# A reordered ending in a fused ViT tower: one layer and a top-2 mixture of experts on one core

## The chip, the core and the metric

The kernel runs on one core of a Trainium2 chip. A core has a matrix engine (TensorE, "PE" in the profile, with its weight loads listed as "PEld"), VectorE ("DVE"), ScalarE ("ACT"), GpSimd ("POOL"), and SyncE ("SP"), which here only starts transfers. The engines run their own instruction streams and wait for one another through semaphores. The metric is the time of one execution on the device in microseconds (us). Before the change it is 2110.49 us, the median of 3 runs from 2110.33 to 2110.68.

## What is computed

The reference, cut to what matters (biases and the small helper functions left out):

```python
# x: (4, 64, 512, 64) = batch, channel, time, series
patches = windows of 16 steps, stride 8, edge-padded by 8      # 64 per series
xf = rfft(patches, norm='ortho')                               # 9 frequencies
h = concat(xf.real, xf.imag) @ W.T                             # (4, 4096, 256)

# layer 0, on a = layernorm(h)
n = layernorm(a);  q, k, v = n @ Wq.T, n @ Wk.T, n @ Wv.T
mem_t = 0.9 * mem_(t-1) + k_t * v_t                            # along the tokens
a = a + q * mem
h = h + a + relu(layernorm(a) @ W1.T) @ W2.T                   # 256 -> 1024 -> 256

# mixture of experts, on tok = layernorm(h)
probs = softmax(tok @ router.T);  the two largest of 8, renormalised
h = h + tok + sum over the two of  weight * (gelu(tok @ w1[e]) @ w2[e])
```

There are 4 x 4096 = 16384 tokens of 256 features, all in float32.

## The kernel before

**Blocks.** The tokens are cut into 32 blocks of 512 (`BLK`; `NS` = 31 is the number of the last). A loop over `i` = 0 to 30 works on three blocks at once: `new` (block i: embedding, first norm, q/k/v, the scan that is called retention, the residual), `mid` (block i-1: the MLP, that is `mlp_in(m)` for eight slices of the hidden layer and `mlp_out` for two halves of the tokens, then the norm that gives `tok`) and `old` (block i-2: the router, then the scattering of its tokens). A written-out ending after the loop (L1287 on) does what is left: block 31 (`last`) from its embedding, block 30 (`mid`) from its MLP, block 29 (`old`) from its router, and the experts of all of them.

**Router and token lists.** `rows` copies a block's tokens into rows with tag fields, `logits` (TensorE) and `choose` (VectorE) find the two best experts, `place` computes for every token the two places in per-expert lists, and `scatter` has POOL write the rows to a buffer in DRAM, `xbuf`: eight indirect transfers per block, two per group of 128 tokens. `scatter(n)` writes up to group n, so a block's scatters can be spread.

**Expert tiles.** After a block's rows are placed, `take(n, block, writes)` (VectorE) makes tiles from the full lists: 256 rows of one expert each. The schedule of tiles is fixed: `take(29)` makes tiles 105 to 108 in the last round of the loop (from block 28), `take(30)` tiles 109 to 112 (block 29) and `take(31)` the last 18, tiles 113 to 130, partly filled (block 30). There are 131. Each passes these methods of class `Tile`:

- `load` (L960): SP starts three transfers: the expert's weights `w` (641.5 KB, at a row read from the table of `take`), the tile's rows transposed as `xh` (DMA_TRANSPOSE) and their tags `xg`. SP waits for the table and for the scatters before them. For the last block's tiles the weights are not loaded (L963).
- `fetch` (L982): for just those tiles, a copy of the expert's weights out of the `bank` in SBUF into `w`, by VectorE for even tiles of a `take` and by ScalarE for odd ones.
- `turn` (L991): ScalarE puts the two halves of the transposed rows together as `xT` (two copies, L995).
- `enter` (L997): eight matmul records on TensorE into PSUM (L1002), then two GELUs by ScalarE (L1010).
- `leave` (L1014): eight matmul records (L1019). `sums` (L1027): VectorE adds the bias and scales by the router's weights, and POOL adds the rows into the output by indirect transfers (L1048).

`expert_step` (`expert_halves` in two parts) runs one step of this small pipeline: `load` of the tile four ahead, `turn` of the next (which is the one that enters in the following step), `enter`, `leave` and `sums` of the one before, `fetch` of the tile four ahead. `slot_halves` (L1158) is the loop's form of it: it does nothing unless more than `LEFT` = 3 tiles stand before `enter`. Weights have five buffers, `xh` six, `xT` two, and the PSUM tiles that `enter` shares with transposes (`p_mm`) two.

**The bank.** All eight experts' weights (8 x 641.5 KB) are loaded once more in the ending, into SBUF that the embedding no longer needs. `load_bank` (L938) is a generator: each `next(weights)` starts one load on ScalarE's own queue. Before the change these stand at the MLP products m = 1, 3, 5 and 7 of block 30, after the last of these products, after `place` of block 29, after the first half of block 30's output product, and after `take(30)`. Block 31's tokens never go through lists: for it, each expert runs over the whole block straight from the bank (class `Expert`, L1081 and L1098), between the remaining tiles.

**What sets the order.** For SP, TensorE, VectorE and ScalarE the order of instructions is the order in which the code is written (`manual_schedule`); POOL's order is the planner's. An instruction that waits therefore holds up everything written behind it on its engine. Where line 305 and line 306 appear, they are `to_features`: four TensorE transposes per half of a block, and the copy out of PSUM by ScalarE. Line 767 is the exponential of `choose` for block 31. Line 608 is the transposes of `residual`.

Of the kernel before, what the change touches and what calls it, by code (L numbers as in the profile page):

```python
# [16 lines left out]
AF = mybir.ActivationFunctionType  # L17
# [19 lines left out]
def vit_tower_kernel(  # L37
# [23 lines left out]
    TT = 4  # L61
# [288 lines left out]
    class Block:  # L350
# [381 lines left out]
        def choose(self):  # L732

            ps = self.lg
            shape = [P, TT, E]

            def wide(a):
                return a.unsqueeze(2).to_broadcast(shape)

            lg = small.tile(shape, F32, name="lg")  # L740
            top = small.tile([P, TT], F32, name="top")
            if self.i == NS:
                first_key = small.tile([P, TT], F32, name="first_key")
            else:
                first_key = self.row.bitcast(F32)[:, :, FIRST]
            turned = small.tile([P, TT, G], F32, name="turned_lg")
            nc.vector.transpose(turned.rearrange("p t g -> p (t g)"), ps.rearrange("p t g -> p (t g)"))
            nc.vector.tensor_reduce(top, turned[:, :, :E], AX.X, ALU.max)
            nc.vector.tensor_tensor(lg, turned[:, :, :E], wide(top), ALU.subtract)
            key = small.tile(shape, F32, name="key")  # L750
            self.oh = oh = small.tile([P, 2, TT, E], F32, name="oh")
            nc.vector.scalar_tensor_tensor(key, lg, 0.0, key0, ALU.is_equal, ALU.mult)
            nc.vector.tensor_reduce(first_key, key, AX.X, ALU.max)
            nc.vector.tensor_tensor(oh[:, 0], key, wide(first_key), ALU.is_equal)
            nc.vector.scalar_tensor_tensor(lg, oh[:, 0], -3.0e38, lg, ALU.mult, ALU.add)
            second = small.tile([P, TT], F32, name="second")
            nc.vector.tensor_reduce(second, lg, AX.X, ALU.max)
            nc.vector.tensor_tensor(key, lg, wide(second), ALU.is_equal)
            nc.vector.tensor_tensor(key, key, key0, ALU.mult)
            nc.vector.tensor_reduce(top, key, AX.X, ALU.max)  # L760
            nc.vector.tensor_tensor(oh[:, 1], key, wide(top), ALU.is_equal)
            dtype = F32 if self.i == NS else BF16
            self.both = small.tile(shape, dtype, name=f"both_{dtype.name}")
            nc.vector.tensor_tensor(self.both, oh[:, 0], oh[:, 1], ALU.add)
            self.ex = small.tile([P, TT], F32, name="ex")
            if self.i == NS:
                nc.scalar.activation(self.ex, second, AF.Exp)
            else:
                nc.gpsimd.tensor_tensor(self.ex, euler, second, ALU.pow)

# [7 lines left out]

        def combine(self):

            diff = small.tile([P, TT], F32, name="diff")
            second = small.tile([P, TT], F32, name="second")
            self.weights(diff, second)
            shape = [P, TT, E]
            self.share = self.both
            nc.vector.tensor_tensor(self.share, self.both, second.unsqueeze(2).to_broadcast(shape), ALU.mult)
            first = self.oh[:, 0]
            nc.vector.tensor_tensor(first, first, diff.unsqueeze(2).to_broadcast(shape), ALU.mult)
            nc.vector.tensor_tensor(self.share, self.share, first, ALU.add)
# [68 lines left out]
    def take(n, block, writes):  # L858
# [40 lines left out]
        expert = small.tile([P, KMAX], F32, name="expert")[:, :k]  # L899
        nc.vector.tensor_reduce(expert, past, AX.X, ALU.add)  # L900
        table = four.tile([P, 2, KMAX], I32, name="table")[:, :, :k]
        if block.i >= NS - 1:
            nc.vector.tensor_scalar(table[:, 0, :], expert, float(E - 1), None, ALU.min)
        else:
            nc.vector.tensor_scalar(table[:, 0, :], expert, float(P), float((E - 1) * P), ALU.mult, ALU.min)
# [47 lines left out]
    class Tile:  # L953
# [6 lines left out]
        def load(self):  # L960
            t = self.t
            self.w = five.tile([P, NW], F32, name="w")
            if self.block.i < NS - 1:  # L963
                wrow = nc.sync.value_load(self.table[:, 0, t : t + 1], min_val=0, max_val=(E - 1) * P)
                nc.sync.dma_start(out=self.w, in_=wex[bass.ds(wrow, P), :])

            def rows():
                row = nc.sync.value_load(self.table[:, 1, t : t + 1], min_val=0, max_val=ROWS - S)
                return xbuf[bass.ds(row, S), :]

            self.xh = six.tile([P, 2 * KD, S], U16, name="xh")
            read = nc.sync.dma_start(out=self.xh, in_=rows().bitcast(U16)[:, : 2 * D], transpose=True)
            unordered("rows", read, self.writes)
            self.xg = twelve.tile([P, 2, RW - D], I32, name="xg")
            read = nc.sync.dma_start(out=self.xg, in_=rows()[:, D:].rearrange("(c p) d -> p c d", p=P))
            unordered("rows", read, self.writes)
# [3 lines left out]
            return self.block.put == TT  # L980

        def fetch(self):  # L982
            if self.block.i >= NS - 1:

                assert len(loaded) == E
                t = self.t
                engine, copy = ((nc.vector, nc.vector.tensor_copy), (nc.scalar, nc.scalar.copy))[t % 2]
                e = engine.value_load(self.table[:, 0, t : t + 1], min_val=0, max_val=E - 1)
                copy(self.w.unsqueeze(1), bank[0][:, bass.ds(e, 1), :])
# [157 lines left out]
    def run(steps):  # L1147
        for _ in steps:
            pass

    def expert_step(**how):
        run(expert_halves(**how))
# [2 lines left out]

    LEFT = 3

    def slot_halves(known, load=True, sums=True):  # L1158

        if len(tiles) - at["enter"] > LEFT and at["enter"] + 2 <= known:  # L1160
            yield from expert_halves(load=load, sums=sums)

    def slot(known, load=True):
# [8 lines left out]
    with tc.manual_schedule(engines=MANUAL):  # L1172
# [3 lines left out]
        for i in range(NS):  # L1176
# [54 lines left out]
            if i:  # L1231
                qkv = new.qkv()
                if old:
                    old.logits()
                    old.choose()
                if i >= EARLY:
                    next(ahead)
                next(qkv)
                next(qkv)
                tile_steps = slot_halves(known, sums=False)  # L1240
                next(tile_steps, None)
                next(qkv)
                if old:
                    writes = old.place(at_once=False)
                    old.scatter(1)
                run(tile_steps)
                if old:
                    old.scatter(2, last_product[0])
                next(qkv)
                advance("sums", at["leave"])  # L1250
                later = slot_halves(known, load=False)
                next(later, None)
                next(qkv)
                new.first_norm()
                for m in range(KD):
                    new.scan(m)
                if EARLY <= i < NB - 2:
                    xs[i + 2] = load_x(i + 2)
                mid.mlp_out(0)
                if old:  # L1260
                    old.scatter(3, last_product[0])
            else:
                xs[i + 2] = load_x(i + 2)
                new.first_norm()
                for m in range(KD):
                    new.retention(m)
# [42 lines left out]
        next(weights)  # L1309
        old.logits()  # L1310
        old.choose()
        expert_step()
        writes = old.place()
        next(weights)
        restore_weights()
        last.first_norm()
        last.retention(0)
        mid.mlp_out(0)
        next(weights)
        take(NS - 1, old, writes)  # L1320
        next(weights)
        mid.mlp_out(1)
        last.retention(1)
        beside = expert_halves(fetch=False)
        next(beside)
        mid.features3()
        mid.rows()
        advance("leave", at["enter"] - 1)
        mid.logits()
        mid.choose()  # L1330
        run(beside)
        expert_step(fetch=False, sums=False)
        writes = mid.place()
        advance("sums", at["leave"])
        expert_step(fetch=False, sums=False)
        last.residual()
        expert_step(fetch=False, sums=False)
        advance("sums", at["leave"])
        expert_step(fetch=False)
        take(NS, mid, writes)  # L1340

        last.features2()
        expert_step(turn=False)
        mid.store()
        last.sum_up()
        for m in range(KH):
            last.mlp_in(m)
            if m == TT - 1:
                advance("turn", at["enter"] + 1)
            if m == KH - 3:  # L1350
                expert_step()
        expert_step()
        last.mlp_out(0, expert_step)
# [107 lines left out]
```

## Time and profile before

| | us |
|---|---|
| median of 3 runs | 2110.49 |
| the profiled execution | 2116.49 |
| its span, first to last instruction | 2114.7 |
| stretch of the loop, 0 to 1853: TensorE busy | 1832.66 of 1853.00 |
| 1853 to 1950 (first part of the ending): TensorE busy | 88.75 of 97.00 |
| 1950 to 2015: TensorE busy | 60.94 of 65.00 |
| 2015 to the end: TensorE busy | 95.00 of 99.70 |
| TensorE's granted clock in these four | 1.00, 0.95, 0.97, 1.00 |
| share of time that the DMA engines were busy in these four | 0.61, 0.81, 0.67, 0.44 |

The profile is of one execution, which took 2116.49 us; all times read in it belong to that one, and they are counted from its first instruction. "Busy" is time in which an engine worked on an instruction; a matmul record that runs at a lower clock is busy longer. The granted clock is the share of full speed at which the chip ran TensorE in that stretch. In a timeline a line has the start and the duration in us, the engine, the source line, the instruction, what it writes and reads, and in square brackets the time for which the engine stood idle before it and what ended that: "<-ACT xT L995" is the instruction of ScalarE at line 995 that wrote `xT`, and "<-issue" means that the profile shows nothing that was waited for. In the tables of stretches each engine has its busy time and its number of instructions in the order PE, PEld, DVE, ACT, POOL; after these stand the granted clock, the DMA share and GB/s. In the stretch from 1853 to 2015 the groups with most idle time before them on TensorE are the tiles' first products:

```profile
L1002 PE MATMUL mm<-xT,w 128*128 128x256 f32 x144 | 38.0, 410 | 6.9 <-ACT xT L995 3.8 <-ACT hT L306 2.4 <-issue 0.7
L1019 PE MATMUL tm<-w,ge 128*128 128x256 f32 x144 | 35.1, 388 | 0.0
```

Here the numbers after the count are the group's busy time in us, the mean of one record in ns, the idle time before the group's records, and the three kinds of release that ended most of it.

### The profile page before, as it was taken

To read this page: it belongs to the slowest core of one execution; us is meant where nothing else is said; L and a number is where in the kernel's file an instruction comes from. 1 tells how busy PE (TensorE), PEld (TensorE's weight loads), DVE (VectorE), ACT (ScalarE), POOL (GpSimd) and SP (SyncE) were. 2 spreads that over 40 slices of the span, in tenths; PEclk is the share of its full clock that TensorE was granted. 3 is DMA by queue.
4 is the path that set the end of the run, shared out by engine and by line. 5 is a ranking of instruction groups with operands and counts; after the bars stand their busy time and mean duration, and the time that the engine had idled before them with its cause. 6 is when DMAs were issued, how large, how long until landed. Compare 5 with 4: busy or idle time off the path is not lost.

```text
span 2114.7 us, 30454 instructions
## 1 busy us (share of the span) xinstructions
PE 2077.4 (98%) x9042; PEld 1576.0 (75%) x9042; DVE 1674.8 (79%) x5179; ACT 1100.8 (52%) x1966; POOL 886.9 (42%) x768
## 2 busy tenths in 40 slices
PE   8999999999999999999999999999999999998999
PEld 5777677777777777777777777787777787676776
DVE  6778888888888888888888888888888888767445
ACT  2344455655545565554556555455665545543453
POOL 1032234444444444544444444444444444535444
PEclk9999999999999999999999999999999999999999
DMA  4031256766676676567667766766776567688653
GB/s 142 4 123 64 80 131 138 160 143 129 134 157 146 155 160 139 125 143 159 156 143 160 150 122 136 157 156 143 163 157 118 138 149 161 138 197 168 91 69 50
DMA packets 424519, 283.21 MB, mean 134 GB/s; under 512 B 355104, under 2 KB 391072, under 8 KB 420256
## 3 DMA queue, kind: packets, MB, share of 16 engines
q1 hardware_dynamic: 373424, 208.35, 42.5%
q0 software_dynamic: 49632, 67.39, 17.8%
q10 hardware_dynamic: 1296, 5.52, 0.8%
q8 instruction: 71, 1.16, 0.2%
q14 instruction: 96, 0.79, 0.1%
HBM read 118.36 MB, written 86.52 MB: 97 GB/s over the span
## 4 chain that ended last, share of the span: by engine, by line
PE 74%; DVE 11%; ACT 5%; DMA 5%; issue 2%; POOL 2%; SPq 1%; another core or an unknown queue 0%; ACTq 0%; DVEq 0%; POOLq 0%
PE tm L650 17%; PE sums L339 13%; PE tm L396 9%; PE sums L524 9%; PE mm L1002 8%; PE tm L1019 8%; DMA turned<-planes 3%; DVE st L263 2%; PE mm L540 1%; ACT planes L318 1%; ACT tokT L332 1%; PE tm L1098 1%; PE mm L1081 1%; PE mm L539 1%; SPq L326 1%
## 5 line engine op out<-in xcount | busy, mean ns | idle before, releaser
L1048 POOL DMA_INDIRECT out<-y,xg x226 | 369.2, 1634 | 432.7 <-DVE y L1038 220.2
L650 PE MATMUL tm<-w_sb,aT 128*128 128x256 f32 x2048 | 454.7, 380 | 0.0
L339 PE MATMUL sums<-hT,w_sb 128*128 128x512 f32 x1024 | 451.7, 593 | 1.3 <-ACT aT L640 1.3
L650 PEld LDWEIGHTS tm<-w_sb,aT 128*128 128x128 f32 x2048 | 386.7, 190 | 57.2 <-DVE z L611 4.8
L819 POOL DMA_INDIRECT xbuf<-row,to x248 | 257.1, 1037 | 294.3 <-DVE ks L560 170.5
L339 PEld LDWEIGHTS sums<-hT,w_sb 128*128 128x128 f32 x1024 | 193.4, 190 | 219.9 <-issue 201.0
L396 PE MATMUL tm<-wu,xv 128*128 128x256 f32 x1280 | 282.5, 379 | 0.0
L318 ACT COPY planes<-zz 128x1024 uint16<-128x1024 uint16 x100 | 99.3, 1041 | 342.0 <-DVE zz L292 342.0
L396 PEld LDWEIGHTS tm<-wu,xv 128*128 128x128 f32 x1280 | 242.7, 190 | 32.7
L1002 PE MATMUL mm<-xT,w 128*128 128x256 f32 x1048 | 252.5, 384 | 6.9 <-ACT xT L995 3.8
L1019 PE MATMUL tm<-w,ge 128*128 128x256 f32 x1048 | 253.4, 385 | 0.0
L1002 PEld LDWEIGHTS mm<-xT,w 128*128 128x128 f32 x1048 | 201.3, 193 | 49.9 <-issue 16.0
L1019 PEld LDWEIGHTS tm<-w,ge 128*128 128x128 f32 x1048 | 195.9, 191 | 31.4 <-issue 2.9
L640 ACT ACTIVATE aT<-sums,vec 128x512 f32<-128x512 f32 x256 | 167.0, 690 | 60.6 <-PE sums L339 59.3
L995 ACT COPY xT<-xh 128x512 uint16<-128x512 uint16 x262 | 182.1, 767 | 24.4 <-DMA xh<-xbuf 15.4
L283 POOL TENSOR_SCALAR rstd<-mv 128x4 f32<-128x4 f32 x62 | 42.0, 678 | 333.2 <-DVE mv L264 296.7
L1010 ACT ACTIVATE ge<-mm,w 128x256 f32<-128x256 f32 x262 | 109.9, 474 | 137.5 <-PE mm L1002 76.3
L1036 DVE TENSOR_TENSOR y<-tm,w 128x512 f32<-128x512 f32 x131 | 90.6, 691 | 97.9 <-PE tm L1019 86.6
L332 ACT COPY hT<-turned 128x512 uint16<-128x512 uint16 x100 | 66.2, 762 | 80.5 <-DMA turned<-planes 80.5
L263 DVE BATCH_NORM_STATS2 st<-h 128x6 f32<-128x256 f32 x256 | 104.8, 409 | 3.3
L332 ACT COPY tokT<-turned 128x512 uint16<-128x512 uint16 x116 | 76.5, 760 | 58.7 <-DMA turned<-row 58.7
L524 PE MATMUL sums<-hT,wqkv_sb 128*128 128x256 f32 x360 | 107.1, 379 | 0.0
(224 smaller groups left out, 3105.4 us busy)
## 6 DMA issues: line engine op xcount, KB each, us to landing
w<-in_wex SPq DMA_DIRECT2D x113, 641.5 KB
xb<-in_x SPq DMA_DIRECT2D x32, 1040.0 KB
out<-h SPq DMA_DIRECT2D x31, 512.0 KB
bank<-in_wex ACTq DMA_DIRECT2D x8, 641.5 KB
xbuf<-row,to POOLq DMA_INDIRECT x248
out<-y,xg POOLq DMA_INDIRECT x226
xh<-xbuf SPq DMA_TRANSPOSE x131
xg<-xbuf SPq DMA_DIRECT2D x131, 4.0 KB
```

Of the source, the lines that this page charges most:

```text
L263: nc.vector.bn_stats(self.st[:, t, :], src[:, t, :])
L332: copy(to[:, 1 - i], self.turned[:, :, i, k, :])
L339: nc.tensor.matmul(ps, lhsT=w[:, k, ts(m, P)], rhs=rhs[:, k, :], start=k == 0, stop=k == KD - 1)
L396: nc.tensor.matmul(ps[:, n, :], lhsT=xv[:, i, j, :], rhs=wu[:, i, j, :], start=j == 0, stop=j == J - 1)
L524: nc.tensor.matmul(g[:, n, :], lhsT=lhsT, rhs=rhs, start=False, stop=True, skip_group_check=True)
L640: nc.scalar.activation(self.aT[:, m, :], ps, AF.Relu, bias=vec[:, MB1 + m : MB1 + m + 1])
L650: last_product[0] = nc.tensor.matmul(ps[:, i, :], lhsT=self.aT[:, k, ts(u * 2 + i, P)], rhs=w2_sb[:, k, :], start=k == 0, stop=k == KH - 1,)
L819: write = nc.gpsimd.indirect_dma_start(out=xbuf, out_offset=bass.IndirectOffsetOnAxis(ap=self.to[:, c, t : t + 1], axis=0), in_=self.row[: ...
L995: nc.scalar.copy(halves[:, :, :, 1 - i], self.xh[:, i * KD : (i + 1) * KD, :])
L1002: nc.tensor.matmul(ps[:, m, :], lhsT=self.w[:, k * D + m * P : k * D + (m + 1) * P], rhs=self.xT[:, k, :], start=k == 0, stop=k == KD - 1,)
L1019: last_product[0] = nc.tensor.matmul(ps[:, c, :], lhsT=self.ge[:, k, ts(c, P)], rhs=w[:, (2 + k) * D : (3 + k) * D], start=k == 0, stop=k ...
L1048: add = nc.gpsimd.indirect_dma_start(out=out, out_offset=bass.IndirectOffsetOnAxis(ap=number[:, c, :], axis=0), in_=y[:, c, :], in_offset= ...
```

## The change

**The exponential.** For block 31, `choose` only keeps `second`, and `combine` begins with the exponential of it.

**Block 29's tiles.** In `take`, `load` and `fetch` the limit `NS - 1` becomes `NS - 2`: tiles 109 to 112 no longer load their weights from DRAM in `load`, and copy them from the bank in `fetch`.

**One more tile in the loop's last round.** `slot_halves` gets a parameter `left`. In round 30 its last use (`later`) takes `LEFT - 1`, so that a tile enters there which before entered in the ending.

**The ending's order.** In block 29's part, the tile between `choose` and `place` goes; block 31's first norm and first half of the retention move ahead of `place`. The second half of the retention moves into block 30's first output product (between its two groups of 128 tokens), and block 31's residual into the second one. After it come a tile, `features2` of block 31 (its transposes), a tile, the first MLP product of block 31, block 30's router with tiles and block 31's second MLP product between its steps, and `take(31)`. Block 30's rows are scattered in two parts. The other six MLP products of block 31 follow, with a tile and `store` and `sum_up` at the fourth, `turn` at the seventh and a tile at the eighth. Before, block 31's residual and `features2` came after `place` of block 30, with four tiles around, and all eight products after `take(31)`.

**The bank's loads.** The first five and the sixth stay at the same calls (m = 1, 3, 5, 7, after the products, after `place` of block 29); the seventh stands after the second half of the retention and the eighth before `take(30)`, where it was behind.

```diff
@@ choose @@
             if self.i == NS:
-                nc.scalar.activation(self.ex, second, AF.Exp)
+                self.second = second
@@ combine @@
+            nc.scalar.activation(self.ex, self.second, AF.Exp)
             diff = small.tile([P, TT], F32, name="diff")
@@ take @@
-        if block.i >= NS - 1:
+        if block.i >= NS - 2:
             nc.vector.tensor_scalar(table[:, 0, :], expert, float(E - 1), None, ALU.min)
@@ Tile.load @@
-            if self.block.i < NS - 1:
+            if self.block.i < NS - 2:
                 wrow = nc.sync.value_load(self.table[:, 0, t : t + 1], min_val=0, max_val=(E - 1) * P)
                 nc.sync.dma_start(out=self.w, in_=wex[bass.ds(wrow, P), :])
@@ Tile.fetch @@
-            if self.block.i >= NS - 1:
+            if self.block.i >= NS - 2:
@@ slot_halves @@
-    def slot_halves(known, load=True, sums=True):
-        if len(tiles) - at["enter"] > LEFT and at["enter"] + 2 <= known:
+    def slot_halves(known, load=True, sums=True, left=LEFT):
+        if len(tiles) - at["enter"] > left and at["enter"] + 2 <= known:
             yield from expert_halves(load=load, sums=sums)
@@ the loop @@
-                later = slot_halves(known, load=False)
+                later = slot_halves(known, load=False, left=LEFT - (i == NS - 1))
@@ the ending @@
         old.logits()
         old.choose()
-        expert_step()
-        writes = old.place()
-        next(weights)
         restore_weights()
         last.first_norm()
         last.retention(0)
-        mid.mlp_out(0)
+        writes = old.place()
+        next(weights)
+        out_steps = mid.mlp_out_steps(0)
+        next(out_steps)
+        last.retention(1)
+        next(weights)
+        run(out_steps)
         next(weights)
         take(NS - 1, old, writes)
-        next(weights)
-        mid.mlp_out(1)
-        last.retention(1)
-        beside = expert_halves(fetch=False)
+        out_steps = mid.mlp_out_steps(1)
+        next(out_steps)
+        last.residual()
+        run(out_steps)
+        expert_step()
+        last.features2()
+        beside = expert_halves()
         next(beside)
+        last.mlp_in(0)
         mid.features3()
         mid.rows()
-        advance("leave", at["enter"] - 1)
+        run(beside)
         mid.logits()
         mid.choose()
-        run(beside)
-        expert_step(fetch=False, sums=False)
-        writes = mid.place()
-        advance("sums", at["leave"])
-        expert_step(fetch=False, sums=False)
-        last.residual()
-        expert_step(fetch=False, sums=False)
-        advance("sums", at["leave"])
-        expert_step(fetch=False)
+        expert_step()
+        writes = mid.place(at_once=False)
+        mid.scatter(2)
+        last.mlp_in(1)
+        expert_step()
+        mid.scatter(TT)
         take(NS, mid, writes)
-
-        last.features2()
-        expert_step(turn=False)
-        mid.store()
-        last.sum_up()
-        for m in range(KH):
+        for m in range(2, KH):
             last.mlp_in(m)
             if m == TT - 1:
+                expert_step(turn=False)
+                mid.store()
+                last.sum_up()
+            if m == KH - 2:
                 advance("turn", at["enter"] + 1)
-            if m == KH - 3:
+            if m == KH - 1:
                 expert_step()
```

## The prediction

> **What bounds the kernel now.** I read the page's busy times first, then TensorE (PE) in order of time for the stretch that the change reorders, then ScalarE (ACT) and the DMA issues of SP for the same stretch.
>
> ```profile
> PE 2077.4 (98%) x9042; PEld 1576.0 (75%) x9042; DVE 1674.8 (79%) x5179; ACT 1100.8 (52%) x1966; POOL 886.9 (42%) x768
> ```
>
> PE is busy for 98% of the span. The change keeps every product (the built programs hold the same ones), so it can move the end only through PE's idle time and PE's slow stretches. In the ending these are (start, duration, instruction, in brackets the idle time before it):
>
> ```profile
> 1911.64 1.89 PE L1002 MATMUL mm<-xT,w 128*128 128x256 f32 x8
> ...
> 1915.01 0.66 PE L305 MATMUL mm<-ident,tok 128*128 128x128 f32 x4 [1.04 <-ACT ge L1010]
> ...
> 1926.36 0.66 PE L608 MATMUL tm<-ident,ret 128*128 128x128 f32 x4 [0.72 <-DVE y L1036]
> ...
> 1931.17 1.99 PE L1002 MATMUL mm<-xT,w 128*128 128x256 f32 x8 [0.70 <-issue]
> ...
> 1938.69 1.11 PE L305 MATMUL mm<-ident,zz 128*128 128x128 f32 x4 [3.36 <-issue]
> 1942.23 3.78 PE L1002 MATMUL mm<-xT,w 128*128 128x256 f32 x8 [2.43 <-ACT hT L306]
> 1945.81 3.01 PE L1019 MATMUL tm<-w,ge 128*128 128x256 f32 x8
> ...
> 2009.97 3.44 PE L1002 MATMUL mm<-xT,w 128*128 128x256 f32 x8 [3.76 <-ACT xT L995]
> ```
>
> The reader sees a middle hole, five waits of 1.04 + 0.72 + 0.70 + 3.36 + 2.43 = 8.25 us, and a late hole of 3.76. Eight such matmuls normally take 1.89; after the long waits they take 3.78, 3.01 and 3.44. The table of stretches has the clock beside it (TensorE's granted clock is the third number from the end):
>
> ```profile
> 1820.00:1824.00 4.00, 1.08 (x8) 0.63 (x4) 3.55 (x17) 2.08 (x5) 1.28 (x1) 1.00 1.20 248
> 1824.00:1828.00 4.00, 3.96 (x12) 3.28 (x13) 3.01 (x6) 3.07 (x7) 3.59 (x3) 0.65 1.08 339
> ...
> 1913.00:1918.00 5.00, 3.96 (x36) 2.93 (x34) 2.93 (x4) 3.62 (x6) 0.00 (x0) 1.00 0.07 27
> ...
> 1939.00:1943.00 4.00, 1.57 (x6) 1.07 (x5) 2.33 (x9) 1.07 (x2) 1.56 (x1) 0.50 1.00 145
> ```
>
> Slow starts in the middle: 0.5 on the four transposes, then by starts 3.58 and 2.85 against 1.73 each, together 3.5 us. The late one: 3.27 from start to start against 1.73, 1.55 us.
>
> ScalarE explains the late hole, and how a transfer can stop it:
>
> ```profile
> 1821.92 1.38 ACT L995 COPY xT<-xh 128x512 uint16<-128x512 uint16 x2 [4.58 <-DMA xh<-xbuf]
> ...
> 2007.14 1.28 ACT L767 ACT_TABLE_LOAD   x1 [5.05 <-DVE second L757]
> 2008.43 0.21 ACT L767 ACTIVATE ex<-second 128x4 f32<-128x4 f32 x1
> 2008.55 1.38 ACT L995 COPY xT<-xh 128x512 uint16<-128x512 uint16 x2
> 2009.94 1.28 ACT L1010 ACT_TABLE_LOAD   x1
> ```
>
> **What goes.** (1) The late hole. PE's next tile waits for xT, which stands in ScalarE's queue behind the exponential, and that waits for VectorE's `second`. Moved into `combine`, two tiles later, the exponential finds `second` ready: 3.76 + 1.55 = 5.31. (2) The middle hole with its slow start, 8.25 + 3.5 = 11.75, as its order is gone. (3) 0.29 before the transposes of line 608 in block 30's round, where an added tile's four products (1.73 us) now cover VectorE. Together 17.35. Entering one tile more there moves 3.46 us of PE work forward and takes it off later: nothing in the sum.
>
> **What comes, step by step on the old clock.** (a) ScalarE at tile 105. Since one tile more has been entered, xT of tile 105 is now copied at block 30's fourth MLP product, right after its load is issued; before, a round later. Its transpose was issued at 1874.10; the copies that feed SP run 1.35 later in my walk, so 1875.45. Landing: 6.39 after issue for the tile of 1815.45, 8.4 for 105 itself (the third bank load waited for it, issued at 1882.52). The middle, 7.4, gives 1882.85; copy and GELU took 2.07 at 1821.92, so 1885.0. Queued behind it are the ReLUs of block 30, the third bank load and hT of block 31, and PE wants the PSUM buffer of that GELU at 1853.18 + 3.46 - 0.29 + 25.67 (embedding to line 305) + 0.44 = 1882.46. PE waits 2.5; the two rows give 1.4 to 3.6, the best case 0, and the 17.8 us of the transpose issued at 1883.90 (the eighth bank load, behind it, left at 1901.95) gives 12.9.
>
> (b) The clock. The 2.96 us gap at 1821 was followed by a clock of 0.65: from 1824.04 to 1829.29 5.25 us for 3.45 of products, 1.8 lost. The 1.04 gap lost nothing (1.00 in 1913 to 1918). 2.5 is nearer to 2.96: 1.8, bounds 0 and 1.8. [...]
>
> (c) Block 31's first retention product now follows the logits without a tile between; its PSUM waits for the last ReLU (0.69): 0.2.
>
> (d) VectorE, counted from t, the end of the first half of block 30's output product. PE needs the normed residual (zz) at t + 11.26 (four groups of 3.45, 0.9, 3.45, 3.46). VectorE: add and statistics 2.0, `take` 3.77 (1901.60 to 1905.37), then the residual chain, 6.45 to the first quarter and 7.45 to the last (1926.88 to 1934.3): last at t + 13.2. Transposes and hT end at t + 13.9 instead of 12.1: 1.8. Then `tok` (0.7 + 1.25 + 2.55 + 1.4 after zz) is out at t + 19.05, wanted with a tile's four products and an MLP product between: 1.3. Then the one-hot for `place`: sums of tiles 104 and 105, the bank copy for tile 109 (0.83) and choose (2.98) stand before it: t + 26.7 against 25.35: 1.35.
>
> (e) Late: from the end of the second tile's first products ScalarE needs GELU 0.73, bank copy 1.15, load, exp, xT, load 4.09 (2007.14 to 2011.23), expert GELU 0.69: 6.66. PE has 1.73 + 3.45 + 1.73 = 6.91 to do. Cost 0, cover 0.25. With no cover each us costs one; the bounds are 0 and 1.3 (one more load exposed). [...]
>
> (f) At nothing: the four weight loads of block 29's tiles leave SP's queue (0.34 us of issue each, 641.5 KB). In exchange VectorE and ScalarE copy two each (0.83, 1.26); the first is in (d), the others run under MLP products. Bank loads: they stay in ScalarE's queue and each waits for a semaphore's previous transfer (the fifth for the weights of tile 107, 10.2 us from 1882.84 to 1893.0 before, the sixth for that tile's transpose). The retention copies behind them have until some 1898 and 1906; by these rows they start at 1895 and 1903. Later costs one for one. Block 30's scatters start some 12 us later and two stand behind an add in POOL's queue; tile 113's transposed rows come 7 us ahead of PE; before it was 16.
>
> New: 2.5 + 1.8 + 0.2 + 1.8 + 1.3 + 1.35 = 8.95. Net 17.35 - 8.95 = 8.4 us. The profiled execution is 2116.49 (span 2114.7 and 1.79 around it), so 2108.1 by its own clock; it stands 6.0 above the median of 2110.49. Some of the waits may belong to the profiled execution alone; I carry the difference over whole: **2102.1**.
>
> **Rivals.** *The transfer is in time.* If tile 105 lands within 4.9 us, (a) and (b) vanish: 4.3 more, 2097.8. For: the third bank load now leaves after that transfer. Against: no landing row here is under 6. *The middle returns what it gave.* Landing after 11 us, or waits in (d) larger by half: 3 to 4 back, 2105.7, and with both 2108; only the late hole remains. For: VectorE's queue decides three steps in a row. Against: its rows repeat within hundredths. *Slower: ScalarE's queue behind the DMA.* Place: xT of tile 105, with block 30's ReLUs behind it. Price: one us per us of landing over 7.4. At 17.8 it is 2112.5; from about 20 (8.4 + 4.2 over) it is slower by over 0.2%; at 22, 2116.7. For: in the trace of before a transfer of the same stretch took 17.8, with DMA share 0.88 from 1853 to 1910. Against: that one was behind five bank loads issued in 7 us, and here two are out. *The change doesn't do what it says*: four of the eight loads stay at the same products and the fifth beside them; the "one by one" alone is worth nothing, and the gain must come from the order and the exponential. This is in the sum already.
>
> **How the numbers follow.** Forecast 0.52 (2099 to 2106), in time 0.18, returned 0.20, slower queue 0.10. Three runs spread over 0.35 us; 0.2%, 4.2 us, is what a measurement tells from no change, so faster means under 2106.3. Faster: 0.52 + 0.18 + 0.03 of the third = 0.73; same 0.17; slower 0.10. Range 2095.5 to 2109: it leaves out the slow queue and the ends of the second and third case.
>
> **What would show it.** PE's late idle time before line 1003 (old 1002) gone and the table load without a wait for `second`; the gap now before line 305 with zz of block 31's first norm, ScalarE's xT ahead of it ended by the DMA, a clock under 1 after it; waits of 1 to 2 us before the zz and tok transposes. Wrong if that gap is over 10 us, if retention waits behind a bank load, or if tile 113 waits for its rows.

## The result and the profile after

The changed kernel is slower: 2119.40 us median of 8 runs (2114.74 to 2123.73) against 2111.03 for before on the same chip (2108.01 to 2114.97), ratio 1.0037, 95% interval 1.0023 to 1.0051. A second set, on another chip, gave 1.0030 (1.0018 to 1.0042), 2122.25 against 2116.88. The forecast was 2102.1 with a range to 2109.0.

The profiled execution of the changed kernel is its run of 2116.52 us, the second lowest of its eight. That its span, 2114.7, is the same as the span of the profile before is chance: before was profiled in a run above its median, the changed kernel in one below.

The first line of the page, engines and busy time:

```profile
PE 2074.8 (98%) x9042; PEld 1574.1 (74%) x9042; DVE 1677.9 (79%) x5181; ACT 1101.7 (52%) x1968; POOL 889.5 (42%) x768
```

It looks as before. The difference is in the chain of waits (start, duration, what), read at its end. Before:

```profile
2103.07 6.93 PE tm L1098 x32
...
2110.03 0.70 DVE zz L1106
...
2110.76 0.48 DVE h L1112
```

After:

```profile
2094.13 5.21 PE tm L1099 x24
...
2099.36 0.70 DVE zz L1107
...
2100.08 0.89 DVE h L1113 x2
...
2101.01 1.55 POOL out L1049
...
2102.86 3.69 DMA out<-y,known
...
2107.33 1.57 POOL out L1049
2108.90 1.86 POOLq L1461
```

Before, the program ends through TensorE and VectorE's last sums. After, it ends through POOL: an indirect add into the output, the landing of it, the next add. TensorE's last product ends at 2101.05 (2109.99 before), 9.7 us ahead of POOL's last add, which ends its issue at 2110.76 (2109.61 before). The four lines behind these numbers, TensorE's and POOL's last, before:

```profile
2106.37 3.62 PE L1098 MATMUL tm<-bank,ret 128*128 128x256 f32 x16
...
2107.83 1.78 POOL L1048 DMA_INDIRECT out<-y,known  x1 [0.30 <-issue]
```

and after:

```profile
2097.43 3.62 PE L1099 MATMUL tm<-bank,ret 128*128 128x256 f32 x16
...
2109.20 1.56 POOL L1049 DMA_INDIRECT out<-y,known  x1 [0.30 <-issue]
```

TensorE did come earlier, and nothing came of it.

The adds are a second chain. `sums` lets the adds of a tile wait until both adds of the tile before have landed, since two experts may hold the same token. In POOL's timeline after, the last links are

```profile
2094.60 1.55 POOL L1049 DMA_INDIRECT out<-y,known  x1 [2.92 <-DMA out<-y,known]
2096.45 1.55 POOL L1049 DMA_INDIRECT out<-y,known  x1 [0.30 <-issue]
2101.01 1.55 POOL L1049 DMA_INDIRECT out<-y,known  x1 [3.00 <-DVE h L1113]
2102.86 1.55 POOL L1049 DMA_INDIRECT out<-y,known  x1 [0.30 <-issue]
```

A link is 1.55 + 0.30 + 1.55 + 3.0, about 6.4 us. (The releaser "DVE h" is only the last event by the profile; the add waits for the landing.) From the first add of block 30's 18 tiles to the first of the last pair it takes 112.6 us after (1994.73 to 2107.33, 17 links of 6.62) and 113.4 before (1992.53 to 2105.96). POOL's 42% busy hides that over the last 110 us each pair of adds waits for the landing of the pair before it.

### The profile page after: what moved, and what is told of

Its sections match the earlier page's. It is cut to its first block, busy times and chain, and to the rows that moved or that the text cites. A ratio compares the mean times of both kernels' runs of the same rounds, so it can differ in the third digit from the quotient of the medians.

```text
span 2114.7 us, 30442 instructions
## 1 busy us (share of the span) xinstructions
PE 2074.8 (98%) x9042; PEld 1574.1 (74%) x9042; DVE 1677.9 (79%) x5181; ACT 1101.7 (52%) x1968; POOL 889.5 (42%) x768
```

## The experiments

Two theories are named in all expectations. Theory A: POOL's chain of adds sets the end after the change, and TensorE's product order no longer does. Theory B: the end is still TensorE's, and the new order costs it time that the one profile doesn't show. All ratios are to before, on the same chip; b_twice and a_expback have 4 executions each, the others 5 to 12. "PE" is the end of TensorE's last product in the run's profile, "POOL" the end of the last add's issue, both in us.

| run | ratio, 95% interval | PE | POOL |
|---|---|---|---|
| b_again (before) | 0.9999, 0.9987 to 1.0011 | 2109.35 | 2110.32 |
| a_again (changed) | 1.0030, 1.0018 to 1.0042 | 2102.41 | 2113.87 |
| b_half | 0.9995, 0.9984 to 1.0006 | 2111.46 | 2104.37 |
| a_half | 0.9981, 0.9972 to 0.9991 | 2101.70 | 2094.62 |
| b_none | 0.9990, 0.9982 to 0.9999 | 2101.94 | |
| a_none | 0.9983, 0.9974 to 0.9993 | 2099.31 | |
| b_twice | 1.0044, 1.0029 to 1.0059 | 2114.46 | 2110.54 |
| a_twice | 1.0037, 1.0026 to 1.0047 | 2110.14 | 2115.55 |
| a_expback | 1.0039, 1.0024 to 1.0054 | 2105.16 | 2116.61 |
| exp_only | 0.9985, 0.9973 to 0.9997 | 2104.71 | 2110.83 |
| exp_again | 0.9999, 0.9986 to 1.0012 | 2100.35 | 2103.69 |
| a_left | 1.0034, 1.0021 to 1.0048 | 2099.26 | 2113.40 |
| f1 | 1.0017, 1.0006 to 1.0028 | 2103.81 | 2113.52 |
| f2 | 1.0027, 1.0014 to 1.0040 | 2101.51 | 2107.32 |
| f2_again | 1.0030, 1.0018 to 1.0042 | 2104.67 | 2115.38 |
| f3 | 1.0009, 1.0000 to 1.0019 | 2104.59 | 2112.46 |
| f4 | 1.0030, 1.0018 to 1.0042 | 2103.60 | 2113.39 |
| b_fix | 1.0010, 0.9999 to 1.0020 | 2107.11 | 2110.98 |

**Second profiles** of both kernels.

> The kernel before once more, for a second profile of it. Theory A (POOL's chain of adds into out sets the end after the change, TensorE's order sets it before): the time is near 2111; TensorE's last product ends after the last add's issue by some us or within 2 us of it, as in the first profile (2109.99 against 2109.61). Theory B (the new order costs TensorE time that the one profile of the changed kernel happens not to show): says nothing of this run.

> The changed kernel once more, for a second profile of it. A: the time is 2115 to 2124; TensorE's last product ends 9 us or more before the last add of POOL is issued and near 2101, as in the first profile, whatever the time is; a longer time lies in longer steps of the chain of adds (over 6.6 us for each tile). B: a run above 2118 shows TensorE's last product above 2106.

As A had it: in the changed kernel TensorE ends 11.5 us ahead of POOL, in before 1.0 ahead, and a run above 2118 shows no TensorE above 2106, against B. Only A's longer steps did not come: the links are 6.63 us, as in the first profile, and the 3.1 us by which this span is longer (2117.8) lie before the chain, whose first add of block 30's tiles comes at 1997.75 and not 1994.73. In four profiles each with TensorE's order untouched, TensorE's last product ends at 2101.94 to 2111.46 in the old order and 2099.31 to 2102.41 in the new.

**Taking the chain away.** Half, then all, of the adds of the last 18 tiles:

```diff
             before = added[-2:] + [self.block.stored]
-            for c in range(2):
+            for c in range(1 if self.block.i == NS - 1 else 2):    # *_half
+            for c in range(0 if self.block.i == NS - 1 else 2):    # *_none
```

> The changed kernel, where each of the last 18 tiles adds only the first 128 of its 256 rows into out (the other half is left out): one link of the chain of adds is then some 4.9 us (1.55 issue, 0.3, about 3 landing) and not 6.6. A: POOL's chain falls behind no more, TensorE sets the end: 2101 to 2107 (before 2111 less the 9 us by which TensorE's last product came earlier). B: 2114 or more, since TensorE's work is as it was.

> The kernel before with the same half of the last 18 tiles' rows left out. A: its end was set by TensorE or by both together, so little goes: 2105 to 2111, and it is slower than the changed kernel with the same left out by 4 to 10 us. B: the changed kernel with the half left out is slower than this one, as the whole one is (by some 8 us).

> The kernel before without any adds for the last 18 tiles (their rows are left out of the output), so that TensorE alone sets the end. A: as with half of them, 0.9985 to 1.000, since TensorE's last product is where it was.

> The changed kernel without any adds for the last 18 tiles. A: TensorE alone sets the end; against b_none the gain is that of TensorE's order, which the forecast put at 8.4 us and the profiles of the halved kernels at 9 (their medians at 3): 0.995 to 0.9965 of before if the forecast's sum is right in most runs, near 0.998 if the medians of the halved ones tell the size. B: slower than b_none.

This decides between A and B. Without the adds the changed kernel falls from 1.0030 to 0.9983, some 10 us; before falls from 0.9999 to 0.9990, some 2 us. So the chain held back the changed kernel by some 10 us and before by some 2. The end of the chain of waits of a_none is TensorE's again:

```profile
2093.90 5.42 PE tm L1099 x25
...
2099.35 0.70 DVE zz L1107
```

The ratios of a_none and b_none are what A gave (near 0.998, the smaller of its two gains for TensorE's order; 0.9985 to 1.000). In us, a_half at 2112.42 (expected 2101 to 2107) and b_half at 2115.66 (2105 to 2111) missed A's, but before itself took 2116.88 on this chip and not the 2111 that A counted from; as differences from before, 4.5 and 1.2 us less, both lie in A's ranges (4 to 10, 0 to 6). The 3.2 us between the two miss A's 4 to 10. With the chain gone the new order is worth 3 us by the medians (3.2 with half, 2.8 with none), in the profiles 2.6 and 9.8. The intervals of a_none and b_none overlap, those of the halved ones too: a gain of TensorE's order is likely but small.

**More work on TensorE**, the first products of two dense experts done twice (6.9 us):

```diff
-                for k in range(KD):
+                for k in list(range(KD)) * (2 if self.e < 2 else 1):
```

> The changed kernel with extra work on TensorE alone: the first products of experts 0 and 1 on block 31 are done twice (16 records more, 6.9 us). Theory A (POOL's chain of adds sets the end; TensorE's last product has some 9 us of slack before it): the time stays within 2 us of the changed kernel's, 1.0030 of before, that is 1.002 to 1.004. Theory B (TensorE's order sets the end): 6.9 us more, 1.006.

> The kernel before with the same 6.9 us on TensorE. A: here TensorE's last product and the last add come together (2109.99 and 2109.61 in the profile, 4.7 and 3.9 us before the end), so most of it shows: 4 to 7 us, 1.002 to 1.0035, and this kernel is then as slow as the changed one. B: 6.9 us, 1.0033.

The changed kernel went from 1.0030 to 1.0037, 1.5 us by the ratios for 6.9 us of work, in A's range; before went to 1.0044, 9 us, more than A's 4 to 7 and more than the work itself, on 4 executions with an interval of 6 to 12.5 us. In the profile of a_twice TensorE's last product still ends 5.4 us ahead of the last add's issue:

```profile
2106.52 3.62 PE L1099 MATMUL tm<-bank,ret 128*128 128x256 f32 x16
```

```profile
2113.99 1.56 POOL L1049 DMA_INDIRECT out<-y,known  x1 [0.30 <-issue]
```

**The exponential**, put back in the changed kernel and moved alone in the old one (the two hunks of the change in `choose` and `combine`, reversed or by themselves).

> The changed kernel with the exponential back in choose, as before. A: TensorE's last product comes some 5 us later (near 2107), which its slack of 10 us holds: the time stays at 1.002 to 1.004 of before. B: 5.3 us more than the changed kernel, 1.0055.

> The kernel before with the exponential moved into combine and nothing else. A: the late idle time of TensorE (3.76) and its slow start (1.55) go and TensorE's last product comes some 5 us earlier, but the adds keep their times, so at most 1 us is gained: 0.9990 to 1.0005. B: the 5.3 us of the forecast's step (1) are gained, 0.9975.

> The kernel before with the exponential alone moved, once more, as it is the one edit that was faster than both kernels (0.9985, interval 0.9973 to 0.9997): 0.997 to 1.000 again. If it comes out above 1.000, its gain is not one that can be told from none.

In the changed kernel it makes 0.09%, inside the intervals, though its profile has TensorE waiting again (2.58 for xT). That is A's range, but the interval of 4 executions reaches 1.0054, close to B's 1.0055. Alone it takes TensorE's late hole away in both profiles, and brings 0.15% in one set of runs and 0.01% in the other: it can't be told from none. The first set was outside A's range too.

**The added tile undone.**

```diff
-                later = slot_halves(known, load=False, left=LEFT - (i == NS - 1))
+                later = slot_halves(known, load=False, left=LEFT)
```

> The changed kernel without the one more tile in the loop's last round (that step takes LEFT again). A: one pair of adds more is in the late chain, 3 to 6.6 us on top of the changed kernel: 1.0045 to 1.006. B: TensorE has the same work, a tile later: within 1 us of the changed kernel, 1.003.

1.0034, close to B's number: A's one link more doesn't show in the time. Its first add of block 30's tiles comes at 1998.06, as in the changed kernel (1997.7, mean of after, a_again, a_twice and a_expback). Counted from the embedding of block 31 it comes after 149.9 us, where those four have 144.2 to 146.2, so most of a link is there; but the embedding itself starts earlier (1848.2, and 1850.5 to 1854.6 in those four). In the built order four scatters stand between two adds where there were six.

**What makes the chain late.** In five profiles of the old order (before, b_again, exp_only, exp_again, b_twice) the first add of block 30's tiles comes at 1991.4 on the mean, in the four of the new one at 1997.7: 6.3 us (5.5 if b_half with 1996.99 and a_half with 1998.01 are counted in), about what the medians differ by (5.4 and 8.4). There is a lag at tile 104, whose adds came at 1921.2 (mean of seven) and now at 1929.3 (mean of six). VectorE's timeline after shows where that one comes from:

```profile
1919.05 1.38 DVE L292 TENSOR_SCALAR zz<-z,mv,rstd 128x256 f32<-128x256 f32 x4
...
1924.68 1.38 DVE L292 TENSOR_SCALAR tok<-h,mv,rstd 128x256 f32<-128x256 f32 x4
...
1926.48 0.69 DVE L1037 TENSOR_TENSOR y<-tm,w 128x512 f32<-128x512 f32 x1
```

and POOL's, what comes of it (the last two lines around six scatters of block 30):

```profile
1927.96 1.62 POOL L1049 DMA_INDIRECT out<-y,xg  x1 [17.77 <-DVE tile_share L1032]
...
1943.85 1.55 POOL L1049 DMA_INDIRECT out<-y,xg  x1 [0.30 <-DVE full L867]
...
1954.40 1.61 POOL L1049 DMA_INDIRECT out<-y,xg  x1 [0.30 <-issue]
```

Tile 104 entered at 1869.44. Its second products wait for the next step of the pipeline, at 1916.69, and its y then stands on VectorE behind the residual's norm and block 30's norm, 8 us; POOL stands idle for 17.77. In the old order a step stood between block 29's choice and its placing, so that tile 104 entered later (1883.83), and its y came at 1921.43. The last of POOL's lines is an add behind six scatters of block 30; it starts 9.0 us after the issue of the add before it has ended (1945.40), where the links at the end have 3.

The lag of tile 104 isn't carried through, though. At tile 105 the two orders are less than 1 us apart (1935.4 and 1936.2 on the means of the same seven and six profiles), at tile 106 the new one is 0.8 us ahead, and at tile 107 it is 5.1 us behind (1950.2 and 1955.3). In the old order all eight scatters of block 30 stand between the adds of tiles 104 and 105; in the new one six stand between those of 106 and 107, and two behind. POOL before, the second add of tile 104 and the first of 105:

```profile
1924.88 1.56 POOL L1048 DMA_INDIRECT out<-y,xg  x1 [0.30 <-DVE share L774]
...
1937.13 1.59 POOL L1048 DMA_INDIRECT out<-y,xg  x1 [0.30 <-DVE tile_share L1031]
```

So both orders pay for the scatters, at different places. Four versions (f2 was run twice) tried to start the chain earlier:

```diff
+        advance("leave", at["enter"])         # f2, f3, f4
+        advance("sums", at["leave"])          # f2, f3, f4
         old.logits()
         old.choose()
+        expert_step()                         # f1, f3, f4 (the one at m == 3 goes)
         restore_weights()
         ...
         last.retention(1)
+        advance("leave", at["enter"])         # f3, f4
+        advance("sums", at["leave"])          # f3, f4
         ...
         last.mlp_in(0)
+        advance("leave", at["enter"])         # f4 (the pair again at m == 2), and
+        advance("sums", at["leave"])          # f4: block 30's scatters at four places
```

> The changed kernel with one expert step put back between the router's choice and the placing of block 29 (its tile enters there, and the rows of the tile before it are added some 30 us earlier), and the step at block 31's fourth MLP product taken out, so that the number of tiles in the ending is the same. A: the whole chain of adds starts one link earlier, some 6.5 us; TensorE's last product stays near 2102 (up to 3 us later, since a cover is moved): 2113 to 2118 where the changed kernel has 2122, 0.998 to 1.001 of before. B: TensorE's work is the same and one cover is gone in the later part, so no gain: 1.003 or more.

> The changed kernel, where the second products and the adds of the tile entered at block 30's fourth MLP product come right after block 30's MLP products, ahead of block 29's router, and not 25 us later behind block 31's residual and block 30's last norm on VectorE; nothing else moves. Theory A (the chain of adds sets the end, and it starts late because this tile's y stands behind these norms on VectorE): one pair of adds leaves the late chain, which starts with the next tile at about the same moment: 4 to 6.5 us less than the changed kernel, 0.9997 to 1.0012 of before. Theory B (TensorE's order sets the end): no change, 1.0025 to 1.004.

> As f2, and the next tile too enters early (after block 29's router) and is added early (after the second half of block 31's retention, where VectorE stood idle), so that two pairs leave the late chain; the step at block 31's fourth MLP product goes, so that as many tiles enter in the ending. A: the last add comes 9 to 13 us earlier than in the changed kernel, near 2102; TensorE's last product is then as late or later, and sets the end together with it: 2109 to 2113 where before has 2117, 0.996 to 0.998. B: no gain, 1.0025 or more.

> f2 once more, for a second profile. Theory A (the chain of adds sets the end; its place is read from the first add of block 30's tiles, which came at 1992.2 on the mean of four profiles with the old order, 1997.7 in four with the new one, and 1992.5 in the first profile of f2): the first add of block 30's tiles again near 1993, and the time 4 to 6 us under the changed kernel's, 1.000 to 1.001. If it is near 1997 again, the early add gains nothing in most runs, and what delays it there is read from POOL's waits (the landing of the adds before it, or the scatters of block 29 behind it).

> f3 (1.0009) with a third tile's second products and adds brought forward (to behind block 31's first MLP product) and block 30's scatters given out over four places of the MLP instead of two. A: the chain starts one more step earlier, by some 4 us: 0.997 to 1.000. If the time stays at 1.001, the chain is held by the scatters that stand between its links, not by its start: six of them still stand between two pairs of adds in the built order.

f3 is faster than the changed kernel (1.0009, to 1.0019, against 1.0030, from 1.0018; the two intervals just touch), f1 at 1.0017 likely; f3 missed A's numbers, and f1 came out between A's and B's. The medians of f2 (1.0027 and 1.0030) are what B had. a_none and a_twice speak against B, so what fails here is the other half of A, that the chain is late because of tile 104. f2 gained in its first profile (first add of block 30's tiles at 1992.54) and a third of that in the second (1995.94), and hardly in its median. In f2 the next tile's adds can't start before its own y (1931.2 and 1934.4, for 1934.0 to 1938.2 in the six profiles of the new order), so only about half of the link is saved. f4, though it brought the most pairs forward, was no better than the changed kernel: its first add of block 30's tiles comes at 1993.26, but its links then take 6.86 us on the mean (6.80 in f1 and f3, 6.62 to 6.69 in the four profiles of the new order).

What sets f1 and f3 apart from f2 and f4 in the built order is that block 30's scatters stand four and four between the pairs there, six and two here; no run changes this alone, so it isn't shown to be the reason.

In f1 the add that was brought forward waited for the landing of the one before it while the bank was being loaded, with block 29's scatters behind it:

```profile
1907.58 1.62 POOL L1049 DMA_INDIRECT out<-y,xg  x1 [11.31 <-DMA out<-y,xg]
```

The last one is the old order with the exponential moved and tile 104's adds brought forward:

```diff
         last.retention(0)
+        advance("leave", at["enter"])
+        advance("sums", at["leave"])
         mid.mlp_out(0)
```

> The kernel before with two edits: the exponential in combine (as in exp_only, 0.9985), and the second products and adds of the tile that enters before the placing of block 29 brought forward, right after the first half of block 31's retention. A: this takes one pair of adds out of the late chain without moving anything else, so the chain ends 4 to 6.5 us earlier, and the exponential has already moved TensorE's last product by 5 us: 0.9960 to 0.9980. B: only the exponential's gain: 0.9985 to 0.9990.

1.0010, no gain, and neither A's number nor B's. Tile 104's adds came at 1908.2, but the next pair at 1938.9 (1937.7 in exp_only): it stands behind block 30's eight scatters in both, so that these, not the number of pairs, set the start there. No version here is shown to be faster than before.

## Why the prediction was wrong

**The step that failed** is the first one: TensorE is busy for 98%, so the change "can move the end only through PE's idle time and PE's slow stretches". True of gains in TensorE's time, not of the end. In the profile before, the last add's issue ended at 2109.61, 0.38 us ahead of TensorE's last product. What follows an add's issue takes 3.9 us (2110.76 to 2114.7, after), what follows the last product 4.7 (2109.99 to 2114.7, before): a second chain with about a microsecond of slack. With these two tails the table gives every span: in all twenty profiles it is the later of "PE" + 4.7 and "POOL" + 3.9, to within 0.3 us (0.6 in a_half), and it is POOL's in every kernel with the new order that makes all its adds.

The prediction read POOL only as a queue for scatters, in (f), and costed it at nothing. No rival named it. The rival on the slower side, which had the chance of 0.10 (ScalarE behind a late transposed load), was not what happened, and the change does do what it says. Nor did any of the three signs come by which the prediction would have known itself wrong: the gap was under 10 us, the copies of the retention did not wait for a bank load, and tile 113 did not wait for its rows. All three look at TensorE's path.

**What goes**, (1) and (2): right. TensorE has no late wait for xT (0.2 us at 2007.63), and the five middle waits are gone.

**What comes** was too small. TensorE's timeline after, and two rows of the table of stretches (the clock is the third number from the end):

```profile
1882.20 1.12 PE L305 MATMUL mm<-ident,zz 128*128 128x128 f32 x4 [5.28 <-ACT ge L1011]
...
1919.52 1.73 PE L305 MATMUL mm<-ident,zz 128*128 128x128 f32 x8 [0.94 <-DVE zz L292]
1921.49 3.54 PE L1003 MATMUL mm<-xT,w 128*128 128x256 f32 x8 [0.24 <-ACT hT L306]
...
1935.47 0.21 PE L797 MATMUL tm<-both_bfloat,rc 128*128 128x32 bf16 x2 [1.76 <-DVE both_bfloat L764]
```

```profile
1882.00:1886.00 4.00, 3.80 (x8) 2.26 (x9) 0.00 (x0) 2.26 (x5) 2.10 (x2) 0.50 1.16 324
...
1922.00:1925.00 3.00, 3.00 (x9) 2.34 (x8) 2.52 (x15) 1.21 (x2) 0.00 (x0) 0.50 0.32 57
```

(a) The place and the releaser were right, the size not: 5.28 and not 2.5 (3.62 to 7.52 in eleven profiles with the added tile). The transposes were issued at 1870.93 and the copy began at 1880.07, 9.1 later (7.4 forecast, from rows of 6.39 and 8.4), and TensorE wanted the buffer 6.0 after the issue, not 7.0. (b) The slow clock behind it took 6.69 us (1882.20 to 1888.89) for 3.87 of work: 2.8, not 1.8. (c) 0.20, as forecast. (d) 0.94 before the transposes of zz (1.8 forecast), nothing before those of tok (1.3), 1.76 before `place` (1.35). Behind the first of these the eight matmuls ran at a slow clock, 3.34 from start to start and not 1.73: 1.6 us, which the forecast did not have. The transposes before them took 1.73 and not 1.04, another 0.7. (e) 0.2 (0 forecast): the table load, the exponential and the copies follow one another on ScalarE; the chain of waits after has the load from 2002.80 for 1.28, the exponential from 2004.09, 0.01 us after the load's end, and the copy from 2004.30. Waits and slow clock together are about 13.5 us where the sum had 8.95. Against the 17.35 that went, some 4 us are left of the 8.4.

From block 31's embedding to TensorE's last product it is 256.98 us before and 250.57 after; with the added tile's 3.46 put back the ending gained 2.95. The added tile itself, put at nothing, was covered in part: with it the embedding starts 1.7 us later (1853.1, mean of eleven profiles, against 1851.4 in eight), not 3.46; that is rough, as the eight alone spread over 6 us. The 8.94 us by which TensorE's last product came earlier in the first pair of profiles agree with the 8.4 by chance; some 4 of them are the loop's, which differs that much from one execution to the next.

**Where the time went**: on TensorE some 3 us were gained by the medians of the kernels without the chain (7 by the means of the four profiles each, which spread more), and they are hidden; on the chain of adds some 5 to 8 were lost. That TensorE's time is hidden is shown by a_none and a_twice, and a_expback agrees. The loss has two parts. Counted from block 31's embedding, the last add's issue ends after 257.5 us in the old order (mean of five profiles, 254.4 to 259.4) and after 261.7 in the new one (mean of four, 260.3 to 263.3), 4.2 us later; and the embedding itself is some 1.7 us later with the added tile. Without that tile in the loop (a_left) nothing is gained: its adds come in the ending then, and the last issue ends 265.2 us after the embedding. That tile 104's adds come later, behind two norms on VectorE, is shown by the timelines; that this makes the 4.2 us is not: at tiles 105 and 106 the orders are level again, and bringing its adds forward gave back four to seven tenths of the whole loss together with other edits (f1, f3), or nearly nothing (f2, f4). How the scatters, the bank's loads and the pace at which tiles enter share these 4.2 us stays open.

## What to carry to other kernels

An engine that is 98% busy is not the only bound: look at what ends last on every engine and queue, and list each chain of dependent transfers with its number of links and the time of one (here 17 links of 6.6 us). If a second chain ends within a microsecond of the first, an edit must move both to gain more than that microsecond, and an edit that helps the first at the cost of the second's start loses. One profile of each kernel isn't enough to size 0.4%: the loop of the old order alone differed by 6 us between executions (embedding of block 31 at 1847.8 to 1853.8 in eight profiles).

## What was not expected of the hardware

The same gap of 0.94 us on TensorE (0.93 to 0.95 in six profiles) was followed by a slow clock in two of them: 0.50 from 1922 to 1925 in the changed kernel's first profile and 0.59 from 1923 to 1926 in a_expback, where the eight matmuls took 3.54 and 3.32 us. In a_again, a_half, a_none and a_twice the eight matmuls took 1.99. All six had a wait of 3.77 to 7.52 us some 35 us earlier. What made the difference between the two and the four is not shown here.

The adds of block 30's tiles landed 3.8 us after their issue in the profile after (median), those of the other tiles 4.8. While the bank was being loaded, POOL waited for a landing for 8.57 us (after, at 1883.59), 10.61 (before, at 1898.94) and 11.31 (f1), where the links at the end have 3; that the loads cause this is not shown.
